# Weight sums stored by SyncE and begun ahead of step 0, six early input products left in PSUM banks, a head of 20 steps and a tail of 12 in pieces of 128 columns

## The chip, the cores and the metric

One core of one Trainium2 chip. The metric is the device time of one execution in microseconds, the median of a few runs. The engines are named as in the profile: PE (TensorE matmuls), PEld (its weight loads), DVE (VectorE), ACT (ScalarE), POOL (GpSimd), SP (SyncE, which here only issues DMAs).

## The reference

An LSTM layer over 512 steps with batch 32, 512 inputs and 512 hidden units, and a residual, all in float32:

```python
xW = jnp.einsum('ntd,dg->ntg', x, Wx) + b            # (32, 512, 2048)
def step(carry, xw_t):
    prev_h, prev_c = carry
    a = xw_t + prev_h @ Wh                            # (32, 2048)
    i, f, o = sigmoid(a[:, :Hd]), sigmoid(a[:, Hd:2*Hd]), sigmoid(a[:, 2*Hd:3*Hd])
    g = tanh(a[:, 3*Hd:])
    next_c = f * prev_c + i * g
    next_h = o * tanh(next_c)
    return (next_h, next_c), next_h
out = x + hs                                          # h of all steps, x the input
```

## The kernel before

A gate bank holds one step's 32 x 2048 gate inputs as 128 partitions (four groups of 32 batch rows, one for each quarter of the hidden units) by 512 columns. `h_part(t)` multiplies the transposed hidden state `ht` with `Wh` into that bank: 16 matmuls of 512 columns with 32 stationary columns each, four at a time side by side in the array (the profile counts each float32 matmul as two). `cell(t)` follows on ACT and DVE: sigmoids and tanh, the new cell state, the new hidden state, and a transpose on DVE that gives the next `ht`. Step t + 1's `h_part` needs it, so PE has nothing of the recurrence to do in between and is given filling work. POOL adds the residual (`oc`), and SP stores it every second step.

The filling work is the input product x Wx + b of other steps. There are two ways to make it.

- Plain (`plain_block`): the product of one step, 4 blocks `c` of 32 matmul records on 256 columns. The bias is added by DVE (`bias_full`).
- Streamed: 20 groups of 24 steps (`GS`, `NG`) go through a bilinear scheme with 20 products for 24 (`R`, tables `U_OF`, `V_OF`, `W_OF`), and each product again through a 7-for-8 scheme (`ROW`). DVE makes the sums of inputs (`u_op`, into `ubuf`), PE the 7 products of a slot out of `ubuf` and `vring` (`emit_matmuls`), ACT and DVE take them out of PSUM (`evacuate`), and DVE joins them (`w_op`, 1024 columns each). The results go through DRAM (`xwd`) and come back one step ahead of their use (`load_xw`, ring `xw`), from where ACT copies them into the gate bank (`seed_step`).

The 20 weight sums V (917 KB each) are made once, at the start, on DVE (`v_add`, three operations each), out of the raw weights in `r1` and four tail sums of each weight block (`tail_sums`, in `cbuf`). They are stored to DRAM (`vdram`, `v_store`) and read again for each group, row by row, into `vring` (three rows deep). Six of them need no sum (`parts` out of `r1` and `cbuf`).

So the run has a head of `HEAD` = 24 steps, whose input products are plain: five (`KEPT`) are made before step 0, straight into the gate banks; 19 more are made during steps 0 to 9, parked in `cbuf`, stored to DRAM (`kept`) and read back like the others. At the same time the V sums are made and stored. From step 10 PE streams group 0, 140 products up to step `HEAD_STEPS` = 20, then two and a third of them a step to the end of the last group at step 475. The last eight steps (`TAIL`) are plain again, made from step 476 on in blocks `c`, two a step, then one. From `SPLIT` = 478 on the gate bank is split in two halves with matmuls of 256 columns, so that the cell of the first half begins before PE is done with the second.

The order on each engine is that of the code (a manual schedule). `jobs` lists which V slots are made in which step; `v_stores` and `flush_v` hold their stores back to the end of the cell; `HEAD_STEPS`, `PLAIN` and `PROD` (assumed costs in ns) share the plain steps and products among the head's steps. Every DMA queue is in order, and a DMA that waits for an engine holds up those behind it. `late_load` loads the raw weights again for the tail, at the steps in `LATE`. `load_seeds` loads bias rows for group 0 through POOL one step after the last plain step, and `late_seeds` sums them on DVE a step later.

Of the kernel before, what the change touches and what calls it, by code (L numbers as in the profile page):

```python
# [23 lines left out]
HEAD = 24  # L24
# [6 lines left out]
KEPT = 5  # L31
AHEAD = 28
STREAM0 = HEAD + GS - AHEAD
SPLIT = 478
LATE = (458, 460, 462, 464, 474, 475)
# [54 lines left out]
def kernel(  # L90
# [41 lines left out]
    kept = dram.tile([HEAD - KEPT, P, W], F32, name="kept")  # L132
# [14 lines left out]
    def x_of(t):  # L147
        return xnat[:, xslot(t // TC), t % TC]

# [18 lines left out]

    def late_load(c, a, b):
# [6 lines left out]
    late_loads = [late_load(0, 0, 4), late_load(1, 0, 4), late_load(2, 4, 6), late_load(3, 4, 6)]  # L176
    late_loads += [late_load(2, 6, 8), late_load(3, 6, 8)]
# [19 lines left out]
    def bank_of(t):  # L197
        if t < KEPT:
            return [gbank[0], gbank[1], xbank[3], xbank[4], xbank[0]][t]
        return gbank[t % 2]  # L200
# [374 lines left out]
    def load_xw(t):  # L575
        dst = xw[:, t % 3]
        if t < HEAD:
            nc.sync.dma_start(out=dst, in_=kept[t - KEPT])
# [142 lines left out]

    def keep(p):
        n = p - KEPT
        dst = parks[n % 6]
        add(dst, park_banks[n % 3], bias_full)
        kept_stores.append(lambda: nc.sync.dma_start(out=kept[n], in_=dst))

    with tc.manual_schedule():
# [15 lines left out]
        for k in range(NJ):  # L744
            nc.sync.dma_start(
                out=wh_sb[:, k].rearrange("p j c -> p (j c)"), in_=wh[:, k * NJ * W : (k + 1) * NJ * W]
            )
        load_x(0, 5, 8)
        load_x(1)
# [12 lines left out]
        for f in tail_sums(0, 4) + tail_sums(4, 8):  # L762
            f()
        for t in range(KEPT):
            add(bank_of(t), bank_of(t), bias_full)
        jobs = {}
        for s in range(R):
            jobs.setdefault(s // 3 if s < 6 else s // 2 - 1, []).append(lambda s=s: v_slot(s))
        jobs.setdefault(9, []).extend([lambda i=i: pair_sum(0, i) for i in range(4)] + [early_seeds])
        dve_jobs = []  # L770

        fill = [("plain", p) for p in range(KEPT, HEAD)]
# [11 lines left out]
        for p in range(TAIL):  # L784
            plain_tail += [(p, c) for c in range(4)]

        for t in range(T):
# [9 lines left out]
            if t == HEAD + 2:  # L797
# [6 lines left out]
            if t == 3:  # L804
                load_x(2)
            if t == 5:
                load_seeds(((4, 3), (5, 1)), nc.sync)
                load_group(0)
            if t + 3 >= KEPT and t + 3 < HEAD + NG * GS and t >= 2:
                if t == 2:  # L810
                    pass
                load_xw(t + 3)

            if t < HEAD_STEPS:
                target = head_work * (t + 1) / HEAD_STEPS
                chunks = []
                while done_work < target - 200 and n_plain < HEAD - KEPT:
                    chunks.append(("plain", KEPT + n_plain))
# [13 lines left out]
                for i, (kind, m) in enumerate(chunks):  # L832
                    if kind == "plain":
                        bank = park_banks[(m - KEPT) % 3]
# [3 lines left out]
                        if i == 0:  # L838
                            cell(t)
                            if t + 1 >= KEPT:  # L840
                                seed_step(t + 1)
                            flush_v()
                        keep(m)
                        if m == HEAD - 1:
                            plains_done = t
                        last = i == plains - 1
                        for _ in range(len(todo) if last else -(-len(todo) // (plains - i))):
                            todo.pop(0)()
                    else:
# [13 lines left out]
                        if i == 0:  # L863
                            cell(t)
                            seed_step(t + 1)
                            flush_v()
                            if t == plains_done + 1:
                                load_seeds(((0, 0), (1, 1), (2, 2)), nc.gpsimd)
                if t >= 9 and not v_stores:
                    load_v_ahead()  # L870
                if t >= 13 and group_loaded == 1 and n_plain == HEAD - KEPT and not dve_jobs and not jobs:
# [36 lines left out]
            for _ in range(0 if t < SPLIT - 2 else 2 if t < SPLIT else 1):  # L908
                if plain_tail:
                    p, c = plain_tail.pop(0)  # L910
                    plain_block(HEAD + NG * GS + p, c, tail_banks[p % 2])
                    if c == 3:
                        kept_late.append(p)
            cell(t)
            for p in kept_late:
                dst = buf_of(take(free_c))[:, 0:2].rearrange("p s c -> p (s c)")
# [54 lines left out]
```

## Time and profile before

| | before |
|---|---|
| median of 3 runs | 3131.02 us (3129.40 to 3131.53) |
| the profiled execution | 3131.05 us, its span 3129.1 us |
| PE busy | 3099.7 us, 99% of the span |
| DVE busy | 2230.4 us, 71% |
| ACT busy | 1453.2 us, 46% |
| granted TensorE clock | 0.998 on average |
| DMA | 766.89 MB, 245 GB/s on average |

The trace's times begin at the first instruction, and the execution's own time is 1.95 us longer than the span. Steps are counted from 0; the start of a step is that of its `h_part`: step 0 at 27.88 us, step 5 at 79.58, step 6 at 88.54, step 10 at 129.92, step 11 at 142.34, step 12 at 160.58, step 20 at 239.92, step 476 at 2961.30, step 511 at 3120.79.

A table of stretches (`windows`) shows for each stretch its length and the busy time of each engine, with the number of instructions in brackets, then the clock, the DMA share and GB/s. PE's length minus its busy time is PE's idle time there.

### The profile page before, as it was taken

Reading aid. Unit: us, or ns where it says so; the run is one execution under the profiler, and the core shown is the slowest. Engines: PE = TensorE matmul, PEld = TensorE weight load, DVE = VectorE, ACT = ScalarE, POOL = GpSimd, SP = SyncE. Lnnn points to the kernel's source line nnn. Section 1 sums busy time; section 2 is a strip of 40 time slices with the busy share of each in tenths; the row PEclk is TensorE's granted clock in tenths of the full one; section 3 lists DMA queues with packets and bytes.
Section 4 is the critical chain, followed back from the end, with each engine's and each line's share of the span. In section 5 each row is a group of like instructions: output and inputs, shape, how many; then the busy total and the mean of one; then the engine's idle time right before and its main releaser. Section 6 shows DMA issues by size and latency. Waiting matters only on the chain.

```text
span 3129.1 us, 108637 instructions
## 1 busy us (share of the span) xinstructions
PE 3099.7 (99%) x43768; PEld 1645.9 (53%) x43768; DVE 2230.4 (71%) x6217; ACT 1453.2 (46%) x5481; POOL 235.6 (8%) x511
## 2 busy tenths in 40 slices
PE   9899999999999999999999999999999999999998
PEld 6544445555555555555555555555555555555465
DVE  5687767677776767676776767676777767776644
ACT  1245444444444444444444444444444444444444
POOL 0000000000000000000000000000000000000010
PEclk9999999999999999999999999999999999999999
DMA  7877787777878778777878777777778787878731
GB/s 280 299 270 264 245 260 252 249 255 244 274 227 263 239 256 257 253 245 257 260 243 270 227 258 246 250 254 259 247 254 265 240 266 227 264 243 267 243 94 36
DMA packets 310822, 766.89 MB, mean 245 GB/s; under 512 B 49392, under 2 KB 92144, under 8 KB 309808
## 3 DMA queue, kind: packets, MB, share of 16 engines
q1 hardware_dynamic: 296800, 740.82, 73.1%
q10 hardware_dynamic: 13280, 18.35, 1.6%
q8 instruction: 345, 5.65, 0.7%
q14 instruction: 157, 1.29, 0.1%
q0 software_dynamic: 240, 0.79, 0.1%
HBM read 577.04 MB, written 182.71 MB: 243 GB/s over the span
## 4 chain that ended last, share of the span: by engine, by line
PE 95%; DMA 2%; DVE 2%; issue 1%; ACT 1%; SPq 0%; POOL 0%; ACTq 0%; DVEq 0%; POOLq 0%
PE gbank L216 52%; PE xbank L487 31%; PE bbank L487 5%; PE xbank L165 2%; PE xbank L216 2%; PE bbank L165 1%; DMA vring<-vdram 1%; DMA xs<-in_L_cond_Wx_dram 0%; DVE cbuf L360 0%; PE gbank L165 0%; DVE prod L235 0%; DMA r<-in_L_cond_b_dram 0%; DMA r<-in_L_cond_Wx_dram 0%; DVE s L236 0%; DMA xnat<-in_x_dram 0%
## 5 line engine op out<-in xcount | busy, mean ns | idle before, releaser
L216 PE MATMUL gbank<-wh_sb,ht 128*32 128x512 f32 (+1 forms) x16288 | 1792.3, 578 | 5.1 <-ACT gbank L595 1.8
L216 PEld LDWEIGHTS gbank<-wh_sb,ht 128*32 128x32 f32 x16288 | 606.8, 110 | 847.7 <-issue 715.5
L487 PE MATMUL xbank<-vring,ubuf 128*32 128x256 f32 (+1 forms) x15464 | 957.3, 365 | 11.9 <-DVE ubuf L395 5.7
L231 ACT ACTIVATE s<-gbank 128x128 f32<-128x128 f32 x984 | 275.9, 281 | 1297.6 <-PE gbank L216 1297.1
L487 PEld LDWEIGHTS xbank<-vring,ubuf 128*32 128x32 f32 x15464 | 584.8, 110 | 379.4 <-issue 190.3
L235 DVE TENSOR_TENSOR prod<-s 128x128 f32<-128x128 f32 x1024 | 293.8, 287 | 633.6 <-ACT s L232 633.5
L360 DVE TENSOR_TENSOR cbuf<-cbuf 128x1024 f32<-128x1024 f32 x410 | 493.1, 1215 | 1.5 <-DMA xwd<-cbuf 0.2
L250 POOL TENSOR_TENSOR oc<-xnat,ht 128x128 f32<-128x128 f32 x504 | 233.7, 464 | 2855.5 <-DVE ht L242 1572.8
L238 ACT ACTIVATE tanh_c<-s 128x64 f32<-128x64 f32 x1024 | 262.3, 256 | 250.9 <-DVE s L236 247.8
L242 DVE STREAM_TRANSPOSE ht<-hbuf 128x64 f32<-128x64 f32 x1022 | 250.9, 245 | 75.4 <-DVE hbuf L240 2.3
L595 ACT COPY gbank<-xw 128x512 f32<-128x512 f32 x473 | 284.4, 601 | 0.1
L236 DVE TENSOR_TENSOR s<-prod 128x64 f32<-128x64 f32 x1024 | 230.4, 225 | 35.2
L533 ACT COPY cbuf<-xbank 128x512 f32<-128x512 f32 x375 | 219.2, 585 | 42.1 <-PE xbank L487 23.7
L240 DVE TENSOR_TENSOR hbuf<-o,tanh_c 128x64 f32<-128x64 f32 x1024 | 212.3, 207 | 25.6 <-ACT tanh_c L238 25.2
L232 ACT ACTIVATE s<-gbank 128x64 f32<-128x64 f32 x984 | 226.3, 230 | 0.0
L543 DVE TENSOR_TENSOR cbuf<-xbank,cbuf 128x256 f32<-128x256 f32 x375 | 153.6, 410 | 71.9 <-ACT cbuf L542 70.0
L487 PE MATMUL bbank<-vring,ubuf 128*32 128x256 f32 (+1 forms) x2704 | 200.6, 356 | 0.6 <-DVE cbuf L539 0.6
L487 PE MATMUL xbank<-vring,xs 128*32 128x256 f32 (+1 forms) x2472 | 174.2, 375 | 0.8 <-DVE cbuf L543 0.5
L487 PE MATMUL xbank<-vring,r 128*32 128x256 f32 (+1 forms) x2480 | 173.2, 372 | 0.1
L539 DVE TENSOR_TENSOR cbuf<-bbank,cbuf 128x256 f32<-128x256 f32 x375 | 151.9, 405 | 3.4 <-PE bbank L487 3.4
L233 ACT ACTIVATE o<-gbank 128x128 f32<-128x128 f32 (+1 forms) x509 | 154.2, 303 | 0.0
L546 DVE TENSOR_TENSOR cbuf<-xbank,cbuf 128x256 f32<-128x256 f32 x375 | 152.3, 406 | 0.0
(94 smaller groups left out, 1742.4 us busy)
## 6 DMA issues: line engine op xcount, KB each, us to landing
vring<-vdram SPq DMA_DIRECT2D x340, 896.0 KB, 6.1
xw<-xwd SPq DMA_DIRECT2D x1920, 64.0 KB, 3.9
xwd<-cbuf SPq DMA_DIRECT2D x222, 512.0 KB, 7.1
out_dram<-oc SPq DMA_DIRECT2D x255, 128.0 KB, 2.9
xnat<-in_x_dram SPq DMA_DIRECT2D x63, 512.0 KB, 5.8
xs<-in_x_grouped_dram SPq DMA_DIRECT2D x10, 1536.0 KB, 10.4
vring<-vdram SPq DMA_DIRECT2D x20, 768.0 KB, 7.1
r<-in_x_grouped_dram SPq DMA_DIRECT2D x10, 1536.0 KB, 10.6
```

What stands on the lines that cost most here:

```text
L216: nc.tensor.matmul(dst[j * B : (j + 1) * B], state["ht"][:, k], m, start=False, stop=True, skip_group_check=True)
L231: nc.scalar.activation(s[:, u, 0:2], g[:, n_, 0:2], AF.Sigmoid)
L232: nc.scalar.activation(s[:, u, 2], g[:, n_, 3], AF.Tanh)
L235: nc.vector.tensor_mul(prod[:, u], s[:, u, 0:2], s[:, u, 2:4])
L236: add(nxt[:, u, 3], prod[:, u, 0], prod[:, u, 1])
L238: nc.scalar.activation(tanh_c[:, HALVES[u]], nxt[:, u, 3], AF.Tanh)
L242: nc.vector.transpose(ht[:, 2 * u : 2 * u + 2].rearrange("p q b -> p (q b)"), hbuf[:, HALVES[u]])
L250: (nc.gpsimd if t < T - 8 else nc.vector).tensor_add(oc[:, tt % 2], x_of(t), ht)
L360: op(c_of(dst), c_of(src), c_of(bb))
L487: nc.tensor.matmul(dst[j * B : (j + 1) * B, cols], left_of(gr, s, r)[:, j * B : (j + 1) * B], vring[:, row % 3, RIGHT[r], cols], start=sta ...
L533: nc.scalar.copy(t[:, 0:4:3], xb.rearrange("p (n c) -> p n c", n=2))
L595: nc.scalar.copy(bank_of(t), src)
```

## The change

- `HEAD` is 20 and the tail 12: four plain steps fewer at the front, four more at the back. `END` = 472 is now the end of the stream (it was step 476), `SPLIT` = 474, and `LATE` moves with them. The tail's input for its first four steps is loaded early, into `seeds_own` (`x_early`, `x_plain`).
- The tail's plain product goes in pieces of 128 columns (`plain_part`, 16 to a step): ten a step in the steps 472 and 473, then five a step. Pairs go as one matmul of 256 columns where they can.
- `HEAD_PLAINS` says which plain steps are made in which step: two a step in 0 to 6, one in step 7. Steps 5 to 10 go straight into banks that the steps before them have left (`STRAIGHT`, `bank_of`), with the bias added in place; 11 to 13 straight into the `xw` ring; only 14 to 19 (`PARKED`) still go through DRAM.
- The V stores are issued by SP instead of ACT, each right after its sum. `V_DIRECT` (the six without a sum) and `V_FIRST` (one sum) come before step 0, the other thirteen in steps 0 to 4 (`V_STEPS`).
- Group 0's inputs and its first bias rows are loaded at step 3 instead of 5. The stream begins in step 7, behind its one plain step, and has 140 products up to step 16.

```diff
-HEAD = 24
+HEAD = 20
+STRAIGHT = 11
+PARKED = 14
-SPLIT = 478
-LATE = (458, 460, 462, 464, 474, 475)
+END = HEAD + GS * NG - AHEAD
+SPLIT = END + 2
+LATE = (454, 456, 458, 460, 462, 470, 471)
+HEAD_PLAINS = ((14, 15), (6, 16), (5, 17), (7, 18), (8, 19), (11, 12), (9, 13), (10,))
+V_DIRECT = (0, 2, 6, 9, 18, 19)
+V_FIRST = (1,)
+V_STEPS = ((3, 4, 5), (7, 8, 10), (11, 12, 13), (14, 15), (16, 17))
...
+    def plain_part(t, c, q, n, bank):
+        ko, ki = divmod(c, 2)
+        a = q % 2 * P
+        for j in range(NJ):
+            nc.tensor.matmul(
+                bank[j * B : (j + 1) * B, q * P : (q + n) * P],
+                x_plain(t)[:, c],
+                raw(ko * 4 + j)[:, 2 * ki + 1 - q // 2, a : a + n * P],
...
     def v_store(s, parts, whole=None):
-        dma = lambda o, i: nc.scalar.dma_start(out=o, in_=i)
+        dma = lambda o, i: nc.sync.dma_start(out=o, in_=i)
...
     def keep(p):
-        n = p - KEPT
+        if p < STRAIGHT:
+            add(bank_of(p), bank_of(p), bias_full)
+            return
+        if p < PARKED:
+            add(xw[:, p % 3], park_bank(p), bias_full)
+            return
+        n = p - PARKED
...
+        for s in V_DIRECT + V_FIRST:
+            v_slot(s)
+        flush_v()
         for t in range(KEPT):
             add(bank_of(t), bank_of(t), bias_full)
...
-                while done_work < target - 200 and n_plain < HEAD - KEPT:
-                    chunks.append(("plain", KEPT + n_plain))
+                for p in HEAD_PLAINS[t] if t < len(HEAD_PLAINS) else ():
+                    chunks.append(("plain", p))
...
-            for _ in range(0 if t < SPLIT - 2 else 2 if t < SPLIT else 1):
-                if plain_tail:
-                    p, c = plain_tail.pop(0)
-                    plain_block(HEAD + NG * GS + p, c, tail_banks[p % 2])
+            due = 0 if t < END else 10 if t < SPLIT else 5
+            while due and plain_tail:
+                p, c, q = plain_tail[0]
+                m = 2 if due > 1 and q % 2 == 0 else 1
+                plain_part(HEAD + NG * GS + p, c, q, m, tail_banks[p % 2])
```

First place: ACT's instructions of the steps 0 and 1 before the change, from the tanh of step 0's cell on. `gbank_73` is step 1's bank and `xbank_69` step 2's; `vdram` is where the V sums go.

```order
L238 ACTIVATE tanh_c<-s_89 128x64 x2
L231 ACTIVATE s_89<-gbank_73 128x128
L232 ACTIVATE s_89<-gbank_73 128x64
L231 ACTIVATE s_89<-gbank_73 128x128
L232 ACTIVATE s_89<-gbank_73 128x64
L233 ACTIVATE o_90<-gbank_73 128x128
L238 ACTIVATE tanh_c<-s_88 128x64 x2
L649 DMA vdram<-r_74 128x3x256
L649 DMA vdram<-cbuf 128x3x256
L649 DMA vdram<-cbuf 128x256
L649 DMA vdram<-vring 128x3x512
L231 ACTIVATE s_88<-xbank_69 128x128
```

And SP's instructions after the change, from the last weight load ahead of step 0 on; `r_74` and `cbuf` as a source are the raw weights and the tail sums, so the three last rows are one V sum that needs none made.

```order
L787 DMA wh_sb<-in_L_cond_Wh_dram 128x2048 x4
L151 DMA xnat<-in_x_dram 128x1024
L151 DMA xnat<-in_x_dram 128x384
L151 DMA xnat<-in_x_dram 128x512
L678 DMA vdram<-r_74 128x3x256
L678 DMA vdram<-cbuf 128x3x256
L678 DMA vdram<-cbuf 128x256
```

The V stores have left the queue in which ACT's gate functions stand, and stand on SP right behind the loads that the start needs, ahead of everything that SP stores in the steps.

Second place: PE where the plain steps end and the stream begins, before the change (steps 9 and 10).

```order
L216 MATMUL gbank_73<-wh_sb,ht_94 32x512 x16
L165 MATMUL bbank<-r_74,xnat 32x256 x32
L165 MATMUL xbank_67<-r_74,xnat 32x256 x32
L216 MATMUL gbank_72<-wh_sb,ht_95 32x512 x16
L487 MATMUL xbank_66<-vring,ubuf 32x256 x8
L487 MATMUL xbank_67<-vring,xs_79 32x256 x8
```

And after it (steps 7 and 8). `ubuf` as an input means that the product waits for a sum that DVE makes; `xs_79` needs none.

```order
L245 MATMUL xbank_69<-wh_sb,ht_94 32x512 x16
L178 MATMUL gbank_72<-r_74,xnat 32x256 x32
L516 MATMUL xbank_66<-vring,ubuf 32x256 x8
L516 MATMUL xbank_67<-vring,xs_79 32x256 x8
L516 MATMUL xbank_66<-vring,ubuf 32x256 x8
L516 MATMUL xbank_68<-vring,ubuf 32x256 x8
L516 MATMUL xbank_67<-vring,xs_79 32x256 x8
L245 MATMUL xbank_70<-wh_sb,ht_95 32x512 x16
```

The first streamed product now follows a plain block, not an `h_part`, and ten products stand in the same step behind that block.

Third place: PE after the stream, after the change (the last piece of step 473, steps 474 and 475). `xbank_66` and `xbank_67` are the two halves of an even step's bank, `gbank_72` and `gbank_73` those of an odd step's, `xbank_69` the bank of the plain step that is being made.

```order
L187 MATMUL xbank_69<-xs_79,seeds_own 32x256 x8
L245 MATMUL xbank_66<-wh_sb,ht_95 32x256 x8
L245 MATMUL xbank_67<-wh_sb,ht_95 32x256 x4
L245 MATMUL xbank_66<-wh_sb,ht_95 32x256 x8
L245 MATMUL xbank_67<-wh_sb,ht_95 32x256 x12
L187 MATMUL xbank_69<-xs_79,seeds_own 32x256 x8
L187 MATMUL xbank_69<-xs_79,seeds_own 32x128 x2
L187 MATMUL xbank_69<-r_74,seeds_own 32x128 x2
L245 MATMUL gbank_72<-wh_sb,ht_94 32x256 x8
L245 MATMUL gbank_73<-wh_sb,ht_94 32x256 x4
```

Before, the filling of such a step was eight matmuls of 256 columns (x8); now four of 128 columns stand behind them in each of 34 steps.

More of the change, by code (lines that the diff above doesn't have):

```diff
@@ L197, in bank_of @@
     def bank_of(t):
-        if t < KEPT:
-            return [gbank[0], gbank[1], xbank[3], xbank[4], xbank[0]][t]
+        if t < 9:
+            g0, g1 = gbank
+            return [g0, g1, xbank[3], xbank[4], xbank[0], g1, g0, xbank[3], xbank[4]][t]
         return gbank[t % 2]
@@ L577, in load_xw @@
         if t < HEAD:
-            nc.sync.dma_start(out=dst, in_=kept[t - KEPT])
+            nc.sync.dma_start(out=dst, in_=kept[t - PARKED])
             return
@@ L720, with park_bank @@
     kept_stores = []
-    def keep(p):
-        n = p - KEPT
+    parked = []
+    def park_bank(p):
+        if p not in parked:
+            parked.append(p)
+        return park_banks[parked.index(p) % 3]
+    def keep(p):
+        if p < STRAIGHT:
[5 more added lines that the diff above has]
+        n = p - PARKED
         dst = parks[n % 6]
-        add(dst, park_banks[n % 3], bias_full)
+        add(dst, park_bank(p), bias_full)
         kept_stores.append(lambda: nc.sync.dma_start(out=kept[n], in_=dst))
@@ L766 @@
         jobs = {}
-        for s in range(R):
-            jobs.setdefault(s // 3 if s < 6 else s // 2 - 1, []).append(lambda s=s: v_slot(s))
-        jobs.setdefault(9, []).extend([lambda i=i: pair_sum(0, i) for i in range(4)] + [early_seeds])
+        for t, ss in enumerate(V_STEPS):
+            jobs.setdefault(t, []).extend([lambda s=s: v_slot(s) for s in ss])
+        jobs.setdefault(6, []).extend([lambda i=i: pair_sum(0, i) for i in range(4)] + [early_seeds])
         dve_jobs = []
-        fill = [("plain", p) for p in range(KEPT, HEAD)]
         HEAD_STEPS = STREAM0
@@ L784 @@
         for p in range(TAIL):
-            plain_tail += [(p, c) for c in range(4)]
+            plain_tail += [(p, c, q) for c in range(4) for q in range(4)]
+        late_halves = []
         for t in range(T):
```

49 lines of the change are left out of this document (30 added, 19 removed).

## The prediction

> **What bounds the kernel now.** First the page: the span, the busy times, and the chain that ended last by engine.
>
> ```profile
> span 3129.1 us, 108637 instructions
> PE 3099.7 (99%) x43768; PEld 1645.9 (53%) x43768; DVE 2230.4 (71%) x6217; ACT 1453.2 (46%) x5481; POOL 235.6 (8%) x511
> PE 95%; DMA 2%; DVE 2%; issue 1%; ACT 1%; SPq 0%; POOL 0%; ACTq 0%; DVEq 0%; POOLq 0%
> ```
>
> PE is the bound, and the change takes no matmul away: 512 `h_part`s, 32 plain steps and 2800 products stay. So it can win only what PE loses, 29.4 us of idle time by the page, and what it loses unseen: a low clock, and idle time inside what counts as busy. Second, the table of stretches, cut at the starts of steps, shows where that is.
>
> ```profile
> core 0: us, PE busy (x) PEld busy (x) DVE busy (x) ACT busy (x) POOL busy (x), PEclk, DMA share, GB/s
> 27.88:79.58 51.70, 51.70 (x807) 38.45 (x801) 29.92 (x72) 7.29 (x36) 2.29 (x5) 1.00 0.72 253
> 79.58:88.54 8.96, 7.15 (x103) 4.50 (x93) 8.44 (x19) 1.85 (x8) 0.00 (x0) 1.00 0.95 309
> 88.54:129.92 41.38, 41.38 (x640) 28.70 (x644) 22.86 (x56) 7.38 (x32) 2.29 (x5) 1.00 0.89 315
> 129.92:142.34 12.42, 9.74 (x142) 4.59 (x136) 8.32 (x20) 4.96 (x15) 1.75 (x4) 1.00 0.95 337
> 142.34:160.58 18.24, 12.89 (x156) 5.40 (x152) 10.07 (x24) 4.13 (x14) 0.91 (x2) 0.81 0.51 161
> 160.58:239.92 79.34, 77.47 (x1157) 37.71 (x1153) 63.36 (x144) 36.53 (x117) 3.67 (x8) 1.00 0.82 288
> 239.92:2890.00 2650.08, 2648.89 (x36752) 1380.81 (x36748) 1945.38 (x5423) 1280.84 (x4777) 204.44 (x444) 1.00 0.78 252
> 2890.00:2961.30 71.30, 68.33 (x956) 35.54 (x949) 49.23 (x143) 33.04 (x128) 5.07 (x11) 1.00 0.82 247
> 2961.30:2967.08 5.78, 5.41 (x64) 2.52 (x65) 4.20 (x10) 2.20 (x11) 1.28 (x1) 1.00 0.37 125
> 2967.08:2972.95 5.87, 5.42 (x65) 2.52 (x65) 5.42 (x11) 1.97 (x10) 1.29 (x1) 1.00 0.89 318
> 2972.95:3102.98 130.03, 129.26 (x2305) 78.18 (x2306) 58.95 (x241) 61.26 (x288) 12.41 (x27) 1.00 0.25 74
> 3102.98:3120.79 17.81, 14.66 (x256) 8.28 (x257) 8.63 (x37) 8.41 (x40) 0.00 (x0) 1.00 0.05 17
> 3120.79:3129.10 8.31, 3.67 (x64) 1.98 (x64) 2.86 (x13) 1.70 (x9) 0.00 (x0) 0.99 0.06 16
> ```
>
> Length minus PE busy: 1.81 us in step 5, 2.68 in step 10, 5.35 in step 11, 1.87 in the steps 12 to 19, 1.19 in the 2650 us of the middle, 2.97 ahead of step 476. In step 11 the clock is 0.81, which costs (1 - 0.81) x 18.24 = 3.5 us more. The head's steps thus lose 11.7 + 3.5 = 15.2 us. The tail: 29 split steps take 130.03 / 29 = 4.48 us each, four without filling 17.81 / 4 = 4.45.
>
> Third, who held PE up there, by the table of waits and the timeline.
>
> ```profile
> PE xbank L487 <- DVE ubuf L395: 5.7, 2, 5.1
> PE gbank L216 <- ACT gbank L595: 1.8, 1, 1.8
> PE xbank L487 <- ACT cbuf L533: 1.7, 2, 1.5
> 141.04 1.75 POOL L700 DMA_DIRECT2D r<-in_L_cond_b_dram  x3
> 150.09 0.42 DVE L704 TENSOR_TENSOR r<-r 128x256 f32<-128x256 f32 x1 [1.59 <-DMA r<-in_L_cond_b_dram]
> 153.62 1.93 PE L487 MATMUL xbank<-vring,ubuf 128*32 128x256 f32 x16 [5.08 <-DVE ubuf L395]
> ```
>
> The long stall of step 11 is one line of causes: POOL issues the late bias rows at 141.04, DVE waits in `late_seeds` until 150.09, its next input sum comes 3.5 us later, and PE waits for that. The 1.7 and 1.8 are ACT, late in its in-order queue behind V stores, and DVE, with four `v_add`s in a step of one plain block.
>
> **The tail.** Rates come from the chain of waits: an `h_part` takes 3.43 us, a plain step 3.45 (0.0539 for each record of 256 columns), and eight records 0.43 or, at 128 columns, 0.22.
>
> ```profile
> 106.04 3.45 PE bbank L165 x64
> 109.50 3.43 PE gbank L216 x32
> 1002.31 0.43 PE bbank L487 x8
> 1002.75 0.22 PE xbank L487 x8
> ```
>
> A split step holds 64 + 16 records, 4.31 us of matmuls, and lasts 4.48; without filling 3.45, and lasts 4.45. So the recurrence sets its length, and 0.17 us of PE are free even where PE counts as busy. With a quarter more filling it holds 64 + 20 = 84, 4.53 us, just over the recurrence's 4.48: PE becomes the bound, barely. The bounds are 4.48, if it all fits into the gap, and 4.48 + 0.22 = 4.70, if the piece simply comes on top; I take 4.53, since the row without filling shows that the filling so far lengthened the step by only 0.03.
>
> The new tail: the steps 472 and 473 with ten pieces (3.43 + 2.15 = 5.58, under their present length) 11.65; 34 steps of 4.53, 154.0; three of 4.45 with little or no filling, 13.4; the last 8.31. That is 187.4, against 167.8 from step 476 now: 19.6 more. Gone ahead of it are four `h_part`s and four plain steps, 4 x 6.88 = 27.5. Net **-7.9 us**, and -9.5 or -2.1 by the bounds.
>
> The Trainium skill (TensorE: Matmul & The Clock Gate, Back-to-back issue gap) speaks against narrow pieces: it gives about 81 ns a matmul of 128 columns in a stream of weight loads and matmuls. By it eight would take 0.65 us, and 34 x 0.43 = 14.6 us would go back. The row above, 0.22 for eight with a weight load each, disagrees, and it is this kernel's own.
>
> **The head.** *Ahead of step 0* DVE gets one `v_add` more, between its last tail sum and the first bias sum, which waits for PE:
>
> ```profile
> 20.95 1.22 DVE L618 TENSOR_TENSOR cbuf<-r,cbuf 128x1024 f32<-128x1024 f32 x1
> 24.73 0.70 DVE L765 TENSOR_TENSOR gbank<-gbank,bias_full 128x512 f32<-128x512 f32 x1 [2.56 <-PE gbank L165]
> 80.49 0.95 DVE L637 TENSOR_TENSOR vring<-r 128x768 f32<-128x768 f32 x1
> 82.56 0.95 DVE L637 TENSOR_TENSOR ubuf<-r,vring 128x768 f32<-128x768 f32 x1
> ```
>
> A `v_add` takes 2.07 us (80.49 to 82.56) and fits into the 2.56 of waiting. Without that gap it would cost those 2.07.
>
> *Steps 0 to 6*, two plain blocks each, last 3.43 + 6.90 = 10.33. At most three `v_add`s fall into one (6.2 us). The cell may be 4.5 us late before PE runs dry, since the blocks give 6.9 us and the cell needs about 2.4, so I cost them at nothing; the 1.81 of step 5 goes, because the one step with a single block, step 7, has no `v_add`. The trace shows 51.70 us of such steps with no idle time. Step 7 starts at 27.88 + 7 x 10.33 = 100.2.
>
> *The V stores.* What SP must move from about 30 us on, before the stream's first rows of `vring` are there, is 18.35 MB of V sums (the row of their queue before: packets, MB, share) and 6.0 MB of parked steps, inputs, output and rows, 24.3 MB, all in one queue.
>
> ```profile
> q10 hardware_dynamic: 13280, 18.35, 1.6%
> 40.00:50.00 10.00, 10.00 (x164) 7.58 (x160) 6.35 (x15) 1.36 (x7) 0.46 (x1) 1.00 0.64 222
> 50.00:60.00 10.00, 10.00 (x164) 7.55 (x158) 6.00 (x16) 1.36 (x7) 0.46 (x1) 1.00 1.00 352
> 60.00:70.00 10.00, 10.00 (x161) 7.50 (x156) 6.87 (x16) 1.36 (x7) 0.46 (x1) 1.00 1.04 360
> ```
>
> At the 352 to 360 of a full queue they take 68 us and land at 98; at the 309 to 315 of the steps 5 to 9, 78 us, at 108. The first product can start at 109.2 (below), so I cost them at nothing; the cover is 1 to 11 us, and each us beyond it costs one. Queued behind the stores on SP are output, inputs and group 0; the output of the steps 0 and 1 is stored after some 12.5 MB of them, near 66 us, while POOL needs that buffer again behind step 4's cell, near 75. ACT loses the stores, and its 1.7 us of stall go.
>
> *Step 7* ends the plain steps. Its one block ends at 107.1; DVE then adds the bias in place and only then makes the first input sum.
>
> ```profile
> 126.47 3.71 PE L165 MATMUL xbank<-r,xnat 128*32 128x256 f32 x64
> 126.77 0.69 DVE L725 TENSOR_TENSOR cbuf<-bbank,bias_full 128x512 f32<-128x512 f32 x1 [1.10 <-PE bbank L165]
> 133.12 2.09 DVE L395 TENSOR_TENSOR ubuf<-xs 128x896 f32<-128x896 f32 x2
> 134.26 1.07 PE L487 MATMUL xbank<-vring,ubuf 128*32 128x256 f32 x16 [0.65 <-DVE ubuf L395]
> ```
>
> By these rows 0.30 from the block's end to DVE, 0.69, and 1.14 from the first sum's start to the product: **2.1 us** of PE idle that step 10 had behind an `h_part` as 0.65. Bounds: 0.65 and 2.1.
>
> *The late bias rows.* Step 8 starts at 107.1 + 2.1 + 4.3 = 113.5, its cell ends 3.43 + 2.4 later, POOL adds and issues near 120.0, and by the 9.05 us of before the last row lands at 129.1, DVE's next sum at 132.6. PE is through step 8 at 113.5 + 3.43 + 7.3 = 124.2, with step 9's `h_part` at 127.7 and six products at 130.3. It waits **2.3 us**, between none (rows landed by 126, DMA being quieter than at 141) and the present 5.35. At 2.3 I count no loss of clock; at 5.35, the 3.5 of before again. The Trainium skill (TensorE: Matmul & The Clock Gate, Part 1) has the clock halved after an idle window of about 3.4 us; the trace agrees, with 1.00 after the gap of 1.81 and 0.81 around that of 5.08.
>
> *Steps 9 to 15.* The stream's DVE work is the same 140 products in fewer, denser steps. Before, DVE is busy 8.32 + 10.07 + 63.36 = 81.8 us in the 110 us of the steps 10 to 19; now some 80 in about 95 (84%, at 0.80 in the row that loses 1.87). I take **4.0** for the 1.87, between 1.9 and 9: DVE is then what is late next.
>
> The head's losses come to 2.1 + 2.3 + 4.0 = 8.4 against 15.2: **-6.8 us**. The steps around the end of the stream keep their order and their 2.97 us; one more load of 256 KB stands in SP's queue there, and the input loads shift by four steps in each group, both under what the middle hides (1.19 idle in 2650).
>
> **Sum.** -7.9 - 6.8 = -14.7, from the profiled execution's 3131.05 (its span 3129.1, and 1.95 around it), which is 0.03 off the median: **3116 us**. About 0.2%, 6.3 us, is what a measurement of this kernel can tell from no change, so the same reaches from 3124.8 to 3137.3.
>
> **Rivals.**
> DVE becomes the head's bound: for it, the 84%, and `w_op`s that hold a store on SP with rows of `vring` behind it; against, that 80% cost only 1.87. It loses 9 instead of 4: 3121; and if the wait for the bias rows stays at 5.35 with its 3.5 of clock, 6.6 more: 3128.
> Narrow pieces cost like wide ones: 0.43 instead of 0.22 for the fifth piece, 4.74 a step, 34 x 0.21 = 7.1 more: 3123. Against it, the 0.22 above.
> The change does not fill the tail: the recurrence and the piece add up to 4.70. That gives back 5.8: 3122. For it, that the piece stands right ahead of the next `h_part`.
> On the other side, the V stores come late: one queue, each sum followed at once by its store, so that SP waits for DVE, and DVE for the buffers of earlier stores, as in the row of 222 GB/s. 24.3 MB then take 109 us and land at 139, 30 us after the first product could start: 3116 + 30 = 3146. It decides from 21 us of lateness on (14.7 + 6.3), rows landing at 130, that is, below 24.3 MB / 100 us = 243 GB/s. For it, that the trace never shows this queue alone with stores; against, the 352 to 360 with the stores in the mix.
>
> **How the numbers follow.** The forecast has 0.66; DVE 0.10, half of it at 3121 and half at 3128; narrow pieces 0.05; the unfilled tail 0.07; late stores 0.08; and 0.04 is for a stall that I don't see and that keeps the time where it is. The forecast's own terms at their low ends (0.65, no wait, 1.9, the tail in its gap) give 3108.5, and idle time in the head's ten streamed steps that counts as busy, if it is the tail's 0.17 a step, 1.7 less, 3107; at their high ends the range goes to 3126, which takes in DVE at 3121 and both tails and leaves out 0.05 + 0.08 + 0.04. Faster: 0.66 + 0.05 + 0.05 + 0.07 = 0.83; the same 0.05 + 0.04 = 0.09; slower 0.08, the late stores.
>
> **What would show it.** Right: no PE idle time in steps 0 to 6, V stores gone from ACT and landed by 108 us, the first streamed product near 109; a wait of some 2 us for `ubuf` in step 7 and in step 9 with the clock at 1.00; split steps of 4.53 us and 187 us from the start of step 472 to the last instruction. Wrong: step 10 starting after 143 (113.5 + 10.7 + 10.3 + 2.3 is 137), rows of `vring` as what PE waits for in step 7, a clock under 1 in steps 8 to 10, split steps over 4.7, or new idle time in the middle.

## The result, and the profile after

The changed kernel takes 3129.18 us (median of 20 runs, 3124.82 to 3133.28), the kernel before in the same set 3130.22 (20 runs, 3127.89 to 3131.89). The ratio is 0.9996, interval [0.9989, 1.0002]: no change that can be measured, against a forecast of 3116 and a range from 3107. In a later set the same kernel had 3124.68 (11 runs, 3121.82 to 3130.55) against 3129.99: 0.9983 [0.9974, 0.9992]. So the change brings 1 to 5 us, not 15. The profiled execution took 3126.34 us, with a span of 3124.6; it is 2.8 us below the median of its set, so what follows shows somewhat more gain than the medians do.

The page of the changed kernel, its span and busy times:

```profile
span 3124.6 us, 109095 instructions
PE 3097.0 (99%) x44032; PEld 1664.7 (53%) x44032; DVE 2232.2 (71%) x6217; ACT 1451.1 (46%) x5483; POOL 234.9 (8%) x511
```

PE's idle time was 29.4 us and is 27.6. The table of stretches tells where it is now: the steps 9 to 15 one by one (step 9 first), then the middle (steps 16 to 451), the 20 steps around the stream's end, and the tail from step 472.

```profile
124.64:140.15 15.51, 12.44 (x164) 5.78 (x160) 10.79 (x25) 3.98 (x15) 0.45 (x1) 0.89 0.57 215
140.15:151.97 11.82, 10.63 (x165) 4.99 (x161) 7.50 (x18) 5.50 (x17) 0.46 (x1) 1.00 0.58 187
151.97:164.30 12.33, 10.75 (x164) 4.90 (x160) 10.19 (x21) 4.73 (x15) 0.46 (x1) 1.00 1.00 358
164.30:175.44 11.14, 10.55 (x165) 5.12 (x160) 7.73 (x20) 5.12 (x16) 0.46 (x1) 1.00 1.01 350
175.44:186.88 11.44, 10.95 (x172) 5.63 (x168) 10.83 (x23) 5.08 (x16) 0.46 (x1) 1.00 0.80 270
186.88:199.38 12.50, 10.69 (x164) 5.57 (x160) 11.61 (x22) 4.94 (x16) 0.46 (x1) 1.00 0.58 217
199.38:209.72 10.34, 10.34 (x164) 5.20 (x160) 7.68 (x20) 5.16 (x16) 0.45 (x1) 1.00 1.00 340
209.72:2811.44 2601.72, 2599.62 (x36052) 1360.55 (x36048) 1912.34 (x5324) 1255.51 (x4687) 199.71 (x435) 1.00 0.81 251
2811.44:2937.14 125.70, 121.75 (x1652) 62.85 (x1649) 83.45 (x242) 57.49 (x217) 9.20 (x20) 0.99 0.83 257
2937.14:3124.60 187.46, 180.85 (x3400) 125.24 (x3400) 89.69 (x346) 83.85 (x395) 16.75 (x33) 1.00 0.25 72
```

The same stretches of the kernel before, whose streamed steps carry numbers four higher:

```profile
239.92:2837.21 2597.29, 2596.97 (x36052) 1354.13 (x36048) 1911.07 (x5325) 1256.18 (x4687) 200.30 (x435) 1.00 0.78 252
2837.21:2961.30 124.09, 120.26 (x1652) 62.22 (x1649) 83.54 (x242) 57.70 (x217) 9.21 (x20) 1.00 0.83 256
2961.30:3129.10 167.80, 158.41 (x2752) 93.48 (x2752) 80.06 (x310) 75.53 (x356) 14.99 (x29) 1.00 0.25 75
```

A streamed head step without loss is 10.34 us (row 199.38); step 13 holds eight records more, 10.77. Both kernels start step 0 at 27.88, and step 16 starts at 209.72, where step 20 of the kernel before started at 239.92. The balance takes the four `h_part`s and four plain steps that the tail got, 27.5 us, from the tail:

| stretch | forecast | measured |
|---|---|---|
| head (first step to step 16) | -6.8 | 181.84 - (212.04 - 27.5) = -2.7 |
| middle | 0 | 2601.72 - 2597.29 = +4.4 |
| around the stream's end | 0 | 125.70 - 124.09 = +1.6 |
| tail | -7.9 | 187.46 - 167.80 - 27.5 = -7.8 |
| sum | -14.7 | -4.5 |

The tail is where it should be. The head gave back 4.1, and the stretches costed at nothing lost 6.0. The 1.6 of these around the stream's end is within what varies: in the other profiles with the same loads there this stretch lasts 122.9 to 126.5 us, against 124.09 in the one profile of the kernel before.

What PE waited for in steps 9 to 15 (engine, tile and line, releaser: us in total, times, longest):

```profile
PE bbank L516 <- DVE cbuf L568: 3.3, 2, 1.8
PE xbank L516 <- issue: 2.4, 1, 2.4
PE xbank L516 <- DVE cbuf L572: 1.2, 1, 1.2
```

The 2.4 is step 9, where the timeline has PE waiting for DVE's next input sum behind `late_seeds` (132.10 to 133.18, PE goes on at 133.29). The others are banks that DVE had not yet emptied. The timeline of step 14 shows why (start, length, engine, line):

```profile
195.42 2.35 DVE L389 TENSOR_TENSOR cbuf<-cbuf 128x1024 f32<-128x1024 f32 x2
197.69 0.42 DVE L575 TENSOR_TENSOR cbuf<-xbank,cbuf 128x256 f32<-128x256 f32 x1
198.03 0.41 DVE L568 TENSOR_TENSOR cbuf<-bbank,cbuf 128x256 f32<-128x256 f32 x1
198.50 0.64 PE L516 MATMUL bbank<-vring,ubuf 128*32 128x256 f32 x8 [1.81 <-DVE cbuf L568]
```

The product before on `bbank` was through at 194.1. The `add` that empties the bank (L568) takes 0.41, but two `w_op`s of 1.2 us (L389), which nobody waits for yet, stand ahead of it.

In the middle PE waits for rows of `vring`, here in step 27. SP's queue ahead of that row holds a load of eight inputs (270.36), which stood elsewhere before the change; the kernel before has no such wait in its middle:

```profile
270.36 1.50 SPq L151 DMA_DIRECT2D xnat<-in_x_dram  x1
273.82 0.37 SPq L595 DMA_DIRECT2D vring<-vdram  x1
281.47 1.07 PE L516 MATMUL xbank<-vring,r 128*32 128x256 f32 x16 [0.98 <-DMA vring<-vdram]
```

The row lands at 281.33, 7.5 us after its issue. Without the load ahead of it (xphase, below) it lands 4.7 us after its issue, at 277.25; with it, but in another execution (again, below), at 280.21, in time.

Around the stream's end, SP's queue, then PE's wait and the steps 466 and 467:

```profile
2887.79 0.39 SPq L405 DMA_DIRECT2D xwd<-xnat  x1
2894.26 0.34 SPq L151 DMA_DIRECT2D xnat<-in_x_dram  x1
2894.69 1.77 SPq L613 DMA_DIRECT2D xw<-xwd  x4
2896.56 0.37 SPq L595 DMA_DIRECT2D vring<-vdram  x1
PE xbank L516 <- DMA vring<-vdram: 2.1, 1, 2.1
2895.18:2903.34 8.16, 6.02 (x84) 2.93 (x80) 7.15 (x19) 4.08 (x14) 0.92 (x2) 1.00 0.99 296
2903.34:2911.06 7.72, 7.72 (x96) 3.70 (x91) 2.65 (x9) 1.90 (x9) 0.00 (x0) 0.78 1.00 292
```

The store from the spare buffer is issued at 2887.79. The load of the last inputs into that same buffer is next and must wait until the store has landed, 6 us; the row of `vring` stands behind it and lands late. PE waits 2.14 us in step 466 and then has the lower clock in 467, 1.7 us more.

### The profile page after: what moved, and what is told of

Its sections match the earlier page's. It is cut to its first block, busy times and chain, and to the rows that moved or that the text cites. A ratio compares the mean times of both kernels' runs of the same rounds, so it can differ in the third digit from the quotient of the medians.

```text
span 3124.6 us, 109095 instructions
## 1 busy us (share of the span) xinstructions
PE 3097.0 (99%) x44032; PEld 1664.7 (53%) x44032; DVE 2232.2 (71%) x6217; ACT 1451.1 (46%) x5483; POOL 234.9 (8%) x511
## 4 chain that ended last, share of the span: by engine, by line
PE 96%; DVE 2%; DMA 1%; ACT 1%; issue 0%; SPq 0%; POOL 0%; DVEq 0%; ACTq 0%
PE gbank L245 53%; PE xbank L516 32%; PE bbank L516 5%; PE xbank L245 3%; PE xbank L187 1%; PE xbank L178 1%; PE gbank L178 1%; DMA vring<-vdram 1%; PE bbank L178 0%; DVE cbuf L389 0%; DVE prod L264 0%; DMA r<-in_L_cond_b_dram 0%; DMA r<-in_L_cond_Wx_dram 0%; DVE s L265 0%; DVE ubuf L424 0%
## 5 line engine op out<-in xcount | busy, mean ns | idle before, releaser
L389 DVE TENSOR_TENSOR cbuf<-cbuf 128x1024 f32<-128x1024 f32 x408 | 491.0, 1216 | 1.4
L568 DVE TENSOR_TENSOR cbuf<-bbank,cbuf 128x256 f32<-128x256 f32 x374 | 151.6, 405 | 3.0 <-PE bbank L516 3.0
```

The costliest lines, as they stand in the source:

```text
L389: op(c_of(dst), c_of(src), c_of(bb))
```

## The experiments

The base of all is the changed kernel. Each step's length comes from that run's profile; where no other number is given, a stretch is compared with the one profiled above.

**again**, nothing altered.

> The changed kernel once more, nothing altered. Its 20 times spread over 8.5 us (3124.8 to 3133.3), those of the kernel before over 4.0. Theory A (a few marginal stalls come and go, each with or without a stretch of lower clock behind it): the steps 0 to 8 and the split steps (4.535 each) come out again within 0.1 us, and the two profiles differ at a handful of steps, by 1 to 3 us each, among them 466 and 467 (8.16 and 7.72 instead of 6.02) and some of the steps 9 to 15. Rival B (a general drift): the difference is spread evenly over the 512 steps, under 0.02 us each. Median expected between 3126 and 3132.

Measured: 3124.68 (3121.82 to 3130.55), 0.9983 [0.9974, 0.9992]. Steps 1 to 8 and the split steps agree within 0.1 us, steps 10 to 15 last 69.69 against 69.57. What differs is a handful: step 9 14.56, step 467 6.03, some middle steps by 0.3 to 0.9; theory A. It had not named the largest one: step 0 lasts 13.28 here, waiting for weights, and in the profiles of this case (without vact, below) step 1 starts anywhere between 36.1 and 39.5 us. That is 3.4 us of spread outside every term of the forecast.

**seeds**, the bias rows issued behind the last plain step:

```diff
-                            if t == plains_done + 1:
-                                load_seeds(((0, 0), (1, 1), (2, 2)), nc.gpsimd)
...
                             plains_done = t
+                            load_seeds(((0, 0), (1, 1), (2, 2)), nc.gpsimd)
```

> The late bias rows are issued on POOL behind the last plain step, in step 7, instead of behind the cell of step 8. Theory A (DVE waits in step 9 for rows issued too late, and PE for DVE): the rows land near 117 instead of 129.7, the waits of DVE for them (0.19 + 2.08 + 1.93) go, step 9 lasts 10.4 to 11.2 instead of 15.51 with the clock at 1.00, and the kernel gains 4 to 5 us. Rival B (DVE's work is what is late, and the stall only moves): DVE still has the 3.3 us of sums on these rows to do in step 9, step 9 gains some 2 us and the steps 10 to 12 lose them again; under 1.5 us in all.

Measured: 3119.59 (3118.26 to 3126.19, 7 runs), 0.9972 [0.9961, 0.9982]. Step 9, and the steps 10 to 15:

```profile
125.89:136.23 10.34, 10.34 (x165) 5.20 (x161) 9.79 (x24) 4.18 (x15) 0.46 (x1) 1.00 0.58 203
136.23:206.11 69.88, 64.08 (x973) 31.39 (x969) 56.65 (x121) 30.55 (x95) 2.75 (x6) 1.00 0.83 287
```

Step 9 has no idle time and the full clock, 5.17 us less, and the steps behind it stay (69.88 against 69.57): nothing comes back, theory A. The profiled execution took 3125.29 all the same, since it lost elsewhere: its step 1 starts 1.3 us later than that of the changed kernel, its middle is 1.8 longer and its end 0.8.

**lastx**, the load of the last inputs one step after its buffer is freed:

```diff
                 free_c.remove(NC)
-                load_x(NCHUNK - 1)
                 last_x.append(t)
+            elif last_x and t == last_x[0] + 1:
+                load_x(NCHUNK - 1)
```

> The load of the last eight inputs into the spare buffer comes one step after the step in which that buffer is freed, instead of in it. Theory A (that load waits on SP for the buffer's own store to land, 2888.2 to 2894.3, and holds the rows of vring queued behind it): the 6 us of waiting on SP go, PE's 2.14 us wait for vring in step 466 goes, the clock of step 467 is 1.00 instead of 0.78, and the steps 466 and 467 last 6.0 each: 3.8 us less. Rival B (the DMA engines are full there, 0.99 busy at 296 GB/s, and the row would be late in any case): the wait for vring stays within 1 us of 2.14, or turns up one or two steps later; under 1 us in all.

Measured: 3122.95, 0.9978 [0.9969, 0.9987]. Its stretch around the end, and step 466:

```profile
2812.10:2933.76 121.66, 119.84 (x1653) 62.54 (x1650) 83.43 (x242) 57.51 (x217) 9.22 (x20) 1.00 0.85 264
2895.84:2901.65 5.81, 5.81 (x84) 3.05 (x80) 4.80 (x14) 3.22 (x11) 0.46 (x1) 1.00 0.86 310
```

4.0 us less than in the profile above, with the DMA engines as busy as before: theory A. Against all the profiles with the loads where they stand in the changed kernel (122.9 to 126.5) it is 1.2 to 4.8; step 466 lasts 6.9 to 9.1 us in them and 5.81 here. Its median is only 1.7 under that of the unaltered kernel beside it. The middle of this profile is 2.2 longer, and the unaltered kernel has step 467 at 7.72 in some executions and at 6.03 in others, so half of what is mended was not there every time.

**pairpool**, group 1's sums of pairs on POOL: `eng = nc.gpsimd if g == 1 else nc.vector` in `pair_sum`.

> The four sums of pairs of group 1 (0.95 us each on DVE, in the steps 13 and 14) are made by POOL. Theory A (DVE is late in the steps 10 to 15, and what it has queued ahead of the additions that free PE's banks is what PE waits for): the steps 13 to 15 together (11.44 + 12.50 + 10.34 and the 11.14 before them) lose 2 to 3 us, the waits for cbuf there shrink. Rival B (DVE's amount of work doesn't matter, only the three or four additions in a row ahead of a bank's release in steps 10 and 11): no change beyond 0.5 us. Rival C (POOL takes so long for them, or slows DVE beside it, that the first sum of inputs of group 1 is late): a new wait for ubuf in step 15 or 16, and a loss of 1 to 4 us.

Measured: 3123.16, 0.9978 [0.9969, 0.9987]. The steps 10 to 15 of this kernel, then a sum of pairs on POOL and a sum of inputs on DVE beside it:

```profile
138.76:208.37 69.61, 63.80 (x973) 31.19 (x969) 55.24 (x115) 30.54 (x95) 11.75 (x10) 1.00 0.83 285
185.04 2.82 POOL L487 TENSOR_TENSOR r<-r 128x768 f32<-128x768 f32 x1
186.75 2.06 DVE L424 TENSOR_TENSOR ubuf<-xs 128x896 f32<-128x896 f32 x1
```

Nothing is gained, as rival B had it, but it doesn't refute theory A: DVE has four sums fewer and is busy 55.24 us against 55.55, since the sums of inputs that run beside POOL's take 2.06 and 2.11 us for 1.08 (row 189.07 of the changed kernel, last section). The work was not taken off DVE; for the question of amount or order this run is inconclusive.

**wops**, the `w_op`s into a step's first batch:

```diff
-                        room["dve"] = m * PROD / 4 * 1.5
+                        room["dve"] = m * PROD / 4 * (2.2 if i == 0 else 0.9)
```

> In the streamed steps of the head DVE's sums of products (1.22 us each, line 389) are queued three at a time in a step's first batch, beside the h_part, and almost none in its second and third batch; their count, and DVE's work in a step, stay within one sum. Theory A (not DVE's amount of work but its order: two or three such sums stand ahead of the additions that free a bank, and PE waits 1.2 to 2.3 us for each): the steps 10 to 15 last together 63 to 65.5 us instead of 69.6, and the waits of PE for cbuf in them are gone; 4 to 6 us less. Rival B (DVE is busy 91% of the time these steps would need, and any order is late somewhere): 69 us again, with the waits at other places. Rival C (three sums ahead of the cell make the next step's h_part wait for ht): waits of gbank for ht in the steps 11 to 15, 1 us each, and under 1 us gained.

Measured: 3124.28, 0.9981 [0.9972, 0.999]. Step 10, and the steps 10 to 15:

```profile
139.03:149.45 10.42, 10.42 (x164) 4.93 (x160) 7.15 (x18) 5.32 (x17) 0.46 (x1) 1.00 0.83 253
139.03:206.50 67.47, 63.92 (x973) 31.33 (x969) 56.44 (x120) 30.49 (x95) 2.75 (x6) 1.00 0.87 298
```

2.1 us less with as much DVE work (56.44 against 55.55): order matters, at half the size expected or less. Step 10 is cured; in the steps 11 to 14 some waits for `bbank` remain, and step 12 lasts 0.6 longer. The median hardly shows it, 0.4 under the unaltered kernel's 3124.68 in the set before: the middle of this profile lasts 2605.97, the longest of all.

**xphase**, the input loads four steps later: `divmod(t + 2, TC)` for `divmod(t + 6, TC)`.

> The loads of eight inputs (512 KB) are issued four steps later, so that against the groups of 24 steps they stand where they stood in the kernel before. Theory A (issued in the third step of a group's third, they and the rows of xw behind them delay rows of vring, which PE waits for in the sixth and twelfth step of a group): the stretch from step 16 to step 452 comes down from 2601.7, 2602.0, 2602.9, 2603.5 and 2604.0 (the five profiles so far) to 2597 to 2599 (it is 2597.3 in the kernel before), and fewer than five steps in it last over 0.3 us too long; 4 to 6 us less. Rival B (such stalls come from the run, wherever the loads stand): 2601 or more again, with the late steps at other places of the groups.

Measured: 3122.31, 0.9976 [0.9967, 0.9985]. The middle, the stretch around the end, and step 466:

```profile
209.35:2806.25 2596.90, 2596.66 (x36052) 1336.04 (x36048) 1912.03 (x5324) 1256.49 (x4687) 200.38 (x435) 1.00 0.79 252
2806.25:2934.98 128.73, 121.90 (x1652) 62.67 (x1649) 83.38 (x242) 57.58 (x217) 9.20 (x20) 0.99 0.82 248
2891.34:2901.18 9.84, 6.01 (x84) 2.92 (x80) 8.11 (x19) 4.08 (x13) 0.92 (x2) 1.00 0.90 274
```

The middle is back at what it was before the change (2597.29), theory A, and the table of waits shows none of PE there any more. Four kernels with this edit have 2596.5 to 2598.1 there, the others 2600.8 to 2606.0. The end lost 3.0 of it: PE waits 3.83 us for `vring` in step 466.

**combo**, seeds, lastx, wops and xphase at once.

> Four edits at once: the bias rows issued in step 7, the last inputs loaded a step later, the sums of products in a step's first batch, the input loads four steps later. Theory A (four separate losses): they add up, 5.2 + 3.8 + 5 + 4.5 = 18.5 us less than the changed kernel's 3124.7 to 3129.2 on the two chips: 3106 to 3111; step 16 starts at 198 to 200 instead of 209.7, from a first step at 27.9. Rival B (what is taken away at one place comes back at another, since DVE and the DMA engines are near full in the head): 3115 or more.

Measured: **3110.88** (3109.91 to 3113.32, 5 runs), 0.9942 [0.9929, 0.9954]. Step 9 is 10.34, steps 10 to 15 67.47, the middle 2598.07, the end 124.07. Stretch by stretch they add up, and it beats both kernels. The single medians do not show as much: they lie 5.1, 1.7, 0.4 and 2.4 under the unaltered 3124.68, 9.6 together, and combo 13.8, though not all in one set; and 2.0 us of this profile's gain is an earlier step 1 (36.2 against 38.22), which none of the edits aims at. Two steps around the end were new: 6.90 and 7.67 in the steps 464 and 465.

**narrow**, all filling in pieces of 128 columns: `m = 1`.

> All filling of the split steps in pieces of 128 columns: 20 narrow records a step instead of 8 wide and 4 narrow. Forecast's theory (a narrow record costs 0.027 us, half a wide one): split steps stay at 4.53 us, 187.4 us from the start of step 472 to the end, no change. Rival B (a narrow record costs as much as a wide one, 0.054): 8 more records' worth, 8 x 0.054 = 0.43 more a step, 4.96 us, some 34 x 0.43 = 15 us slower. The Trainium skill (TensorE: Matmul & The Clock Gate, Back-to-back issue gap) gives about 81 ns a matmul of 128 columns; by it the 20 records would take 1.6 us and a split step 5.1, 19 us slower in all.

Measured: 3125.07, 0.9988 [0.9979, 0.9997]. **wide**, whole pieces only: `due = ... 8 if (t - SPLIT) % 4 == 3 else 4`.

> The tail of twelve steps with whole pieces of 256 columns: two pieces a split step, and four in every fourth step, so that the filling is the same in all. Forecast's theory (a step is bound by the larger of the recurrence, 4.45 to 4.48 us, and PE's matmuls, 3.45 + 0.0539 for each wide record): three steps of 4.48 and one of 5.2 (96 records of 0.054), 4.65 on average against 4.53, some 34 x 0.12 = 4 us slower. Rival B (the pieces' size doesn't matter, the filling simply comes on top of a part of the recurrence): 4.53 on average again, no change within 0.5 us in the tail.

Measured: 3128.27, 0.9994 [0.9985, 1.0003]. One split step of the changed kernel, of narrow, and two of wide:

```profile
2975.99:2980.53 4.54, 4.54 (x93) 3.27 (x92) 2.46 (x10) 2.13 (x10) 0.46 (x1) 1.00 0.23 60
2971.70:2976.24 4.54, 4.54 (x112) 3.52 (x108) 2.46 (x10) 2.13 (x10) 0.46 (x1) 1.00 0.26 72
2975.36:2979.81 4.45, 4.45 (x84) 2.52 (x81) 2.43 (x10) 2.14 (x10) 0.46 (x1) 1.00 0.25 66
2979.81:2984.99 5.18, 5.18 (x100) 3.69 (x100) 2.15 (x11) 2.46 (x12) 0.46 (x1) 1.00 0.26 73
```

In a step 32 narrow records in place of 16 wide ones cost nothing (the 39 steps from 472 to 510 take 0.34 us more): a narrow record is half a wide one. Wide pieces lengthen these steps by 3.44 us, since three steps gain 0.08 and the fourth loses 0.65. So 3.4 of the tail's 7.8 come from cutting the pieces finely, the rest from having twelve steps to fill with.

**vact**, the V stores on ACT again: `nc.scalar.dma_start` in `v_store`.

> Part of the change undone: the V sums are stored by ACT again, everything else as changed. The forecast put SP at no cost (their rows land by 108 us, the first product needs them at 109) and gave the stores' leaving ACT 1.7 us, for a cell that came late behind them. Theory A (as forecast): the steps 0 to 6 lose 0 to 4 us, where ACT's cell stands behind stores that wait for DVE; steps from 9 on unchanged; 0 to 4 us slower. Rival B (SP's queue with the stores in it delays what follows, the loads of group 0 and the first rows of vring): with the stores on ACT step 7 (13.35 us) or step 8 (11.03) gets shorter by 0.5 us or more.

Measured: 3154.79 (3152.49 to 3155.43), 1.0073 [1.0057, 1.0088]: 25 us slower than the kernel before and 26 to 30 than the changed one, outside both. What PE and ACT wait for there:

```profile
PE gbank L245 <- DMA wh_sb<-in_L_cond_Wh_dram: 11.0, 4, 5.6
PE xbank L245 <- DVE ht L271: 8.0, 1, 8.0
PE xbank L178 <- DMA xnat<-in_x_dram: 4.1, 1, 4.1
ACT s L260 <- DMA vdram<-ubuf: 33.3, 3, 17.2
```

On SP the first stores are queued behind the loads of `wh_sb` and the inputs; on ACT's own queue they start at 10.3 us and run beside them, and PE waits 15 us in all for what step 0 needs. The clock is at half there for 20.5 us, and step 0 lasts 29.27 us. Later the cell stands behind stores that wait for earlier stores out of the same buffers, and the steps 1 to 8 take 10.2 us more.

**best**, combo with `LATE` at 468 instead of 462, and 3.0 and 0.4 for 2.2 and 0.9.

> The kernel with the four edits, with two more: hardly any sum of products (1.22 us on DVE) outside a head step's first batch, and the load of the inputs of steps 500 to 503 issued in step 468 instead of 462. Theory A (order on DVE, and what stands on SP ahead of rows of vring): the additions that free bbank come earlier, the steps 11 to 14 together 1 to 3 us less than the 46.7 of the four edits; the steps 464 and 465 (6.90 and 7.67 there) 6.0 each, 2.5 us less; 3107 to 3109 where the four edits had 3110.9. Rival B (with the order mended DVE's amount of work bounds the steps 11 to 14; by the order of instructions and the trace's durations it is 10.9 us a step there against the 10.34 of PE): 46 us or more again in these four, and the gain only at the end of the stream.

Measured: 3111.6 (3109.88 to 3115.51, 5 runs), 0.9939 [0.9926, 0.9951]. **bestpool**, the same with pairpool.

> The kernel before this one in the list, with the four sums of pairs of group 1 (3.8 us of DVE in the steps 13 and 14) on POOL, where they took 2.7 us each and slowed DVE's sums beside them from 1.08 to 2.06. Rival B of that kernel (DVE's amount of work bounds the steps 11 to 14): now the same edit that brought nothing before gains 1.5 to 3 us in the steps 13 and 14 (23.7 in the four edits, 20.7 without loss). Theory A alone (order): no change within 0.7 us. A loss of 1 us or more would say that POOL's sums take from DVE as much as they save.

Measured: **3110.31** (3109.99 to 3113.87, 5 runs), 0.9936 [0.9924, 0.9949]. The steps 9 to 15 of combo, best and bestpool:

```profile
122.63:200.44 77.81, 74.25 (x1133) 36.66 (x1129) 66.16 (x143) 34.67 (x109) 3.21 (x7) 1.00 0.83 286
123.37:202.89 79.52, 74.43 (x1132) 36.58 (x1128) 66.59 (x143) 34.56 (x109) 3.19 (x7) 1.00 0.82 283
122.50:201.48 78.98, 74.43 (x1132) 36.58 (x1128) 64.41 (x139) 34.56 (x109) 11.19 (x11) 1.00 0.82 285
```

The later load works: the end lasts 121.95 against 124.07. Four `w_op`s in one first batch are too many: step 11 rises to 12.58 from 11.33, since the cell comes late behind them. So the steps 11 to 14 last 47.3 us, over the 46 of rival B, but for a reason of order. POOL's sums gain 0.5 us in the steps 13 and 14 (22.76 to 22.23): under the 0.7 of theory A, and short of the 1.5 to 3 of rival B. The three kernels can't be told apart by their times. These steps take 72.8 us without loss, so 5 to 7 are still lost in them under each order tried; whether another order, or less work on DVE, would take them away stays open.

## Why the prediction was wrong, by its steps

- **The tail** was right in mechanism and size: -7.8 for -7.9, split steps of 4.54 for 4.53, 187.46 us for 187.4. By narrow, the row of 0.22 us for eight records was the right price. The Trainium skill (TensorE: Matmul & The Clock Gate, Back-to-back issue gap) gives about 81 ns a matmul of 128 columns, by which the estimate for the eight was 0.65; narrow does not bear that out.
- **Steps 0 to 7 and the V stores** were right: no idle time in the steps 0 to 6, step 7 at 100.26 (100.2) with 1.82 us of it (2.1), step 8 at 113.61 (113.5), the stores landed by 92.1 us. That they cost nothing hid what they bring: by vact, 26 to 30 us hang on the move to SP in this head, where the forecast put 1.7.
- **The late bias rows**: the mechanism and the waiting were right. The last row was there at 129.7 (129.1), the product that waits for DVE's next sum began at 133.3 (132.6), and PE waited 2.44 us (2.3). The step that failed is "at 2.3 I count no loss of clock": the clock was 0.89 over step 9, which costs 0.11 x 15.51 = 1.7 us, and a second stall of 0.63 followed. 5.2 in all, as seeds shows.
- **"Steps 9 to 15 ... I take 4.0"** was a term of the right kind and too small: 5.7 us of idle time in the steps 10 to 15, counted as the forecast counted its 1.87 and 4.0, or 7.1 against steps without loss (69.57 - 62.5). It was argued from DVE's share of 84%, and another order of the same work took away 2.1 (wops): part of it is what stands ahead of an `add` that frees a bank. How much of the rest is amount isn't settled, since pairpool didn't lower DVE's busy time, and bestpool lowered it by 2.2 us (66.59 to 64.41) for 0.5 us gained.
- **"The steps around the end of the stream keep their order and their 2.97 us ... the input loads shift by four steps in each group, both under what the middle hides"** is the step that failed outright: +4.4 in the middle, and a stall of 2.14 us with 1.7 of clock at the end, where the stretch as a whole can't be told from the one before (+1.6). The 1.19 us of idle time in 2650 were read as slack, but they said only that the loads fitted where they stood. (Of the 4.4, only 1.8 shows as idle time of PE, 2.10 against 0.32.) Moved by four steps they stand ahead of rows of `vring` in SP's queue (xphase gives the 4.4 back), and the load of the last inputs met its buffer's own store (lastx gives 4.0 back).

With the four edits of combo the changed kernel is 18.6 us under the kernel before (3129.46 in that set): the layout can bear what the forecast promised, and lost it at the three places named. Two of the forecast's own signs of being wrong came: a clock under 1 in step 9, and new idle time in the middle. None of its named rivals happened as described; what came is what it gave 0.04, a stall that it did not see and that keeps the time where it is. Of the named ones the nearest, DVE as the head's bound with 9 us, had about the size of what the head gave back. What is left open: why the medians of the same kernel lie 4.5 us apart in two sets. The start and the marginal stalls vary from run to run, but no run shows what sets them.

## What to carry to other kernels

A moved load can cost what is queued behind it on its queue, even where PE had no idle time before: list for every DMA that shifts against the stream which transfer now stands behind it, and what its own buffer still waits for. On an engine that works in order, ask not how busy it is but what stands ahead of the one instruction that frees a bank. And undo a part that you costed at little: the store queue, priced at 1.7 us, carried 26 to 30.

## What the runs showed of the hardware

Gaps of PE in the steps from step 7 to the stream's end, over all profiles: after those of 0.9 to 1.83 us the clock stayed at 1.00; after thirteen of the sixteen between 1.99 and 5.08 us it fell to half for 3.4 us, which costs 1.7 (around the one of 5.08, in the kernel before, for 6.8 us); after three, of 2.08, 2.36 and 2.66, it did not. Steps 466 and 467 of seeds (2.91 us gap) and of the unaltered kernel's second profile (2.66) show the two cases: 8.93 and 7.72 us, and 8.68 and 6.03. The Trainium skill (TensorE: Matmul & The Clock Gate, Part 1) lets the clock fall after an idle window of about 3.4 us that runs freely; the length of the slow stretch and that the same gap may or may not trip it agree, but here gaps of 2 us suffice, and the forecast had read the rule as a gap of 3.4.

POOL's four sums of 128x768 took 1.82, 1.84, 2.69 and 2.82 us where DVE takes 0.95, and beside the last of them DVE's sum of inputs took 2.06 (pairpool, above): it ends at 188.81, 0.95 after POOL's, as if it had run only then. The same sum in the changed kernel, with POOL idle:

```profile
189.07 1.08 DVE L424 TENSOR_TENSOR ubuf<-xs 128x896 f32<-128x896 f32 x1
```

The Trainium skill (SBUF — State Buffer, Who interferes with whom) says that a VectorE instruction with two inputs in SBUF contends with a GpSimd instruction that reads SBUF. The trace agrees: 1.08 became 2.06.
